# Folding a batch norm's scale into the product that turns a tile, with its biases added to x on GpSimd

## The chip, the cores and the metric

The kernel runs on one core of a Trainium2 chip. The metric is the device time of one execution in microseconds; the median of three runs is given. Names of the engines in the profile: PE is TensorE (PEld its weight loads), DVE is VectorE, ACT is ScalarE, POOL is GpSimd, SP is SyncE, which here only issues transfers.

## What is computed

A graph with 6250 nodes of 256 features and 100000 edges goes through an attention layer and then through three GIN layers. Cut to what matters around the change:

```python
h = relu(layernorm(x))
a = attention(h, edges)            # weights per edge, sums per node
h = batch_norm(h + a @ Wo + bo, bn1_g, bn1_b)
h2 = relu(h @ W1 + b1) @ W2 + b2
x = x + batch_norm(h + h2, bn2_g, bn2_b)      # bn2: this and the next line
h = relu(layernorm(x))                        # are the changed stage
for w, b in ((w1, b1), (w2, b2), (w3, b3)):   # GIN, relu after the first two
    h = ((1 + eps) * h + segment_sum(h[src], dst)) @ w + b
out = x + h
```

The batch norm takes its mean and variance over the nodes, one pair for each feature, and is then one multiplication and one addition: h * r2 + m2, with r2 and m2 a number for each feature.

## The kernel before

The program first sorts out the edges into 53 chunks and computes the first layer norm and the three projections (stage 0); then it runs the function `chunked`:

- attention, chunk by chunk, with rows gathered by indirect transfers that GpSimd issues (`gather`, L396). Its result is `h_t`, kept in SBUF with the features on the partitions: 128 partitions, two halves of the features (index f), 6250 nodes along the free dimension;
- the dense stage (L811 to L835), in 13 parts of up to 512 nodes, that rewrites `h_t` in place and collects the statistics of the second batch norm;
- `batchnorm("bn2", ...)` (L795 to L807), which leaves `r2` and `m2`, one column for each half of the features;
- the changed stage (L838 to L863), called s1c here;
- three passes over the 53 chunks, one for each GIN layer. In each, `neighbours` gathers 15 tiles of 128 rows for a chunk (L893, issued at L396) and sums them with a one-hot product on PE (L894). The first pass reads the table `g0_d` in DRAM, which s1c writes.

s1c works on ten blocks of 5 x 125 = 625 nodes. A block's x is loaded with one row of 256 features for each node (`xg`: 125 partitions, 5 rows each, 3 buffers). `h_t` has the features on the partitions, so each tile of 125 nodes has to be turned: for each half f, ACT computes hn = h_t * r2 + m2 (L847), PE transposes hn against the identity `ident` into the PSUM tile `tp` (L854, 4 buffers), and DVE adds `tp` to `xg` (L855). `layernorm` then takes bn_stats and bn_aggr for each of the five rows on DVE (L150, L151), a square root on ACT and a reciprocal on DVE (L141, L142) and one scalar_tensor_tensor on DVE (L154). ACT writes relu(x * r + m) to `g0` (L860, five times). `xg` goes to `x1_d` and `g0` to `g0_d`.

Every load and store of a block is issued by `halves` (L129 to L132) in two parts, 112 and 13 partitions (SPLIT = 112), 560 and 65 KB. Loads of x and stores of x1 are issued by SP, stores of g0 by ACT. A scheduler sets the order in which each engine gets its instructions; within one engine they run in that order. For SP in s1c it is: loads of blocks 0 and 1; store 0; the large part of load 2; store 1; the small part of load 2; load 3; load 4; stores 2 and so on, with a load waiting until its buffer, used three blocks before, has been stored and read.

Of the kernel before, what the change touches and what calls it, by code (L numbers as in the profile page):

```python
# [27 lines left out]
FT = mybir.dt.float32  # L28
BF = mybir.dt.bfloat16
I32 = mybir.dt.int32  # L30
AF = mybir.ActivationFunctionType
OP = mybir.AluOpType
# [5 lines left out]
P = 128  # L38
NN = 6250
NE = 100000  # L40
D = 256
# [4 lines left out]
FB = 125  # L46
# [41 lines left out]
def gnn_kernel(ctx: ExitStack, tc: tile.TileContext, a: dict, out: bass.AP):  # L88
# [266 lines left out]
    with branch.Else():  # L355
        chunked(tc, a, out, t)
# [3 lines left out]
def chunked(ctx, tc, a, out, t):  # L360

    nc = tc.nc
    iota, iota_p, ident = t.iota, t.iota_p, t.ident
# [431 lines left out]
    def batchnorm(name, stats):  # L795

        g = column(wp, name + "_g", a[f"L0_gnn_{name}_g"], 2)
        b = column(wp, name + "_b", a[f"L0_gnn_{name}_b"], 2)
        mv = wp.tile([P, 2, 2], FT, name=name + "_mv")
        for f in range(2):  # L800
            nc.vector.bn_aggr(mv[:, f, :], stats[:, f].rearrange("p c k -> p (c k)"))
        r = t.rsqrt(wp, name + "_r", mv[:, :, 1], 2)
        nc.vector.tensor_tensor(r, r, g, op=OP.mult)
        m = wp.tile([P, 2], FT, name=name + "_m")
        nc.vector.tensor_tensor(m, mv[:, :, 0], r, op=OP.mult)
        nc.vector.tensor_tensor(m, b, m, op=OP.subtract)
        return r, m  # L807

    r1, m1 = batchnorm("bn1", stats1)
    with tc.tile_pool(name="s1b", bufs=2) as sp, tc.tile_pool(name="s1b_ps", bufs=4, space=PSUM) as pp:  # L810
        for n, (c0, w) in enumerate(parts):  # L811
# [4 lines left out]
            for f in range(4):  # L816
                ps = pp.tile([P, 512], FT, name="ps")
                for k in range(2):
# [4 lines left out]
                        start=k == 0,  # L823
                        stop=k == 1,
                    )
                nc.scalar.activation(hid[:, f, :w], ps[:, :w], AF.Relu, bias=b_1[:, f : f + 1])
            for f in range(2):
# [6 lines left out]
                nc.vector.scalar_tensor_tensor(to, ps[:, :w], b_2[:, f : f + 1], to, op0=OP.add, op1=OP.add)  # L834
                nc.vector.bn_stats(stats2[:, f, n, :], to)  # L835

    r2, m2 = batchnorm("bn2", stats2)
    with tc.tile_pool(name="s1c", bufs=2) as sp, tc.tile_pool(name="s1c_ps", bufs=4, space=PSUM) as pp:  # L838
        for b0 in range(0, NFB, 5):
            xg = sp.tile([P, 5, D], FT, name="xg", bufs=3)  # L840
            halves(nc.sync, lambda s: xg[s], lambda s: rows_of(a["x"], b0, 5)[s])
            for k in range(5):
                b = b0 + k
                hn = sp.tile([P, 2, FB], FT, name="hn")
                tp = pp.tile([P, D], FT, name="tp")
                for f in range(2):
                    nc.scalar.activation(  # L847
                        hn[:, f, :],
                        h_t[:, f, b * FB : (b + 1) * FB],
                        AF.Identity,  # L850
                        bias=m2[:, f : f + 1],
                        scale=r2[:, f : f + 1],
                    )
                    nc.tensor.transpose(tp[:FB, f * P : (f + 1) * P], hn[:, f, :], ident)  # L854
                nc.vector.tensor_tensor(xg[:FB, k, :], xg[:FB, k, :], tp[:FB, :], op=OP.add)  # L855
            r, m = t.layernorm(sp, [xg[:FB, k, :] for k in range(5)], 5)
            halves(nc.sync, lambda s: rows_of(x1_d, b0, 5)[s], lambda s: xg[s])
            g0 = sp.tile([P, 5, D], FT, name="g0")
            for k in range(5):
                nc.scalar.activation(  # L860
                    g0[:FB, k, :], xg[:FB, k, :], AF.Relu, bias=m[:FB, k : k + 1], scale=r[:FB, k : k + 1]
                )
            halves(nc.scalar, lambda s: rows_of(g0_d, b0, 5)[s], lambda s: g0[s])  # L863
# [926 lines left out]
```

## Time and profile before

| what | us |
|---|---|
| median of three runs | 5583.78 |
| their lowest and highest | 5550.34, 5595.96 |
| the profiled execution, device time | 4526.41 |
| its span, first to last instruction | 4524.6 |
| mean granted TensorE clock in it | 0.803 |
| dense stage, 1217 to 1395 | 178 |
| s1c, 1395 to 1478 | 83 |
| the three passes, 1478 to 4524 | 3046 |

The profiled execution is shorter than the timed runs by 1057 us. A profile shows one execution, and all durations below come from it. PEclk is the clock that TensorE was granted, as a share of the full one; a row such as "x100 | 42.6, 571 | 34.0" gives the number of instructions, their busy time in us, the mean of one in ns, and the idle time of the engine just ahead of them with what ended it. Buffer numbers are left out of names, and where a helper issues a transfer, its line is the helper's (L132 for all of `halves`).

### The profile page before, as it was taken

What the parts mean: (1) busy time and instruction counts of PE and PEld (TensorE: products, weight loads), DVE (VectorE), ACT (ScalarE), POOL (GpSimd) and SP (SyncE); (2) the same over time, 40 slices, a digit from 0 to 9 for tenths busy, and PEclk for the clock granted to TensorE, in tenths of its full rate; (3) what the DMA queues carried; (4) which work ended last, traced back from release to release, by engine and by line L of the source; (5) the groups of instructions that cost most, each with busy time, mean ns of one, the idle gap of its engine ahead of it and who ended that gap; (6) DMA issues with size and microseconds to landing.
All of it is one profiled execution on the core that took longest, in us unless ns stands there. A gap on an engine that the chain in (4) does not pass through costs nothing. (4 is left out here: it accounts for less than half of the span.)

```text
span 4524.6 us, 36719 instructions
## 1 busy us (share of the span) xinstructions
PE 3645.1 (81%) x11051; PEld 1912.4 (42%) x11051; DVE 1486.8 (33%) x3034; ACT 746.2 (16%) x1610; POOL 3020.7 (67%) x3186
## 2 busy tenths in 40 slices
PE   7666666666696678877887899999999888888888
PEld 4344444444444334433333344444444333333333
DVE  6577777777724111111111121212121111111110
ACT  2244444444326000000000001010101000000000
POOL 0277777777300777777776777777776677777776
PEclk9888888888896787788777999999999666555555
DMA  4555555555205444444443777777776333333333
GB/s 126 145 150 152 152 152 153 152 152 152 68 1 159 148 126 125 126 126 126 126 126 114 224 243 232 242 231 243 231 243 202 100 112 112 112 112 112 112 112 104
DMA packets 315949, 671.18 MB, mean 148 GB/s; under 512 B 79412, under 2 KB 166734, under 8 KB 315743
## 3 DMA queue, kind: packets, MB, share of 16 engines
q0 software_dynamic: 178080, 524.47, 39.6%
q1 hardware_dynamic: 114005, 126.08, 9.2%
q10 hardware_dynamic: 23658, 18.21, 1.4%
q8 instruction: 89, 1.46, 0.1%
q14 instruction: 117, 0.96, 0.1%
HBM read 614.38 MB, written 54.13 MB: 148 GB/s over the span
## 5 line engine op out<-in xcount | busy, mean ns | idle before, releaser
L894 PE MATMUL sum<-g,hot 128*128 128x256 f32 (+1 forms) x4770 | 2282.1, 598 | 385.0 <-DMA g<-g_d,src_t 236.1
L396 POOL DMA_INDIRECT g<-g_d,src_t x1590 | 1510.5, 950 | 788.0 <-issue 491.9
L894 PEld LDWEIGHTS sum<-g,hot 128*128 128x128 f32 x4770 | 983.2, 240 | 1593.3 <-DMA g<-g_d,src_t 576.2
L396 POOL DMA_INDIRECT g<-vs_d,src_t x795 | 755.9, 951 | 431.7 <-issue 221.0
L396 POOL DMA_INDIRECT g<-y_d,src_t x795 | 753.8, 948 | 274.0 <-issue 233.5
L696 PE MATMUL acc<-g,hot 128*128 128x264 f32 x1590 | 509.5, 466 | 62.7 <-DVE g L686 61.5
L696 PEld LDWEIGHTS acc<-g,hot 128*128 128x128 f32 x1590 | 343.1, 232 | 127.2 <-DVE g L686 74.3
L413 DVE TENSOR_TENSOR hot<-ruler,loc_t 128x1920 f32<-128x1920 f32 x159 | 341.6, 2150 | 11.9 <-DMA g_d<-g 10.0
L1012 DVE TENSOR_TENSOR o<-sum,base 128x256 f32<-128x256 f32 (+1 forms) x53 | 22.5, 425 | 868.3 <-PE sum L894 868.3
L525 PE MATMUL flip<-ident,s_e 128*120 128x128 f32 x53 | 24.7, 465 | 343.3 <-ACT s_e L520 343.3
L686 DVE TENSOR_TENSOR g<-g,at_ps 128x1024 f32<-128x1024 f32 x212 | 239.5, 1151 | 14.9 <-ACT at_ps L677 8.5
L936 DVE SCALAR_TENSOR_TENSOR own<-own,eps,sum 128x256 f32<-128x256 f32 (+1 forms) x53 | 25.5, 480 | 525.6 <-PE sum L894 525.6
L966 PE MATMUL h_ps<-tt,g_w 128*128 128x512 f32 (+1 forms) x448 | 190.8, 570 | 0.6 <-ACT tt L954 0.6
L525 PEld LDWEIGHTS flip<-ident,s_e 128*120 128x120 f32 x53 | 9.2, 174 | 353.7 <-ACT s_e L520 353.7
L1000 DVE SCALAR_TENSOR_TENSOR own<-own,eps,sum 128x512 f32<-128x512 f32 (+1 forms) x53 | 39.5, 746 | 347.4 <-PE sum L894 347.4
L918 ACT COPY tt<-tp 128x256 f32<-128x256 f32 (+1 forms) x53 | 19.7, 372 | 736.5 <-PE tp L917 736.5
L925 DVE TENSOR_TENSOR g<-h_ps,g_b 128x512 f32<-128x512 f32 (+1 forms) x53 | 36.7, 692 | 304.1 <-issue 273.1
L954 ACT COPY tt<-tp 128x512 f32<-128x512 f32 (+1 forms) x53 | 31.0, 585 | 611.3 <-PE tp L953 581.0
L985 DVE SCALAR_TENSOR_TENSOR base<-y,eps,x 128x256 f32<-128x256 f32 (+1 forms) x53 | 25.5, 486 | 315.0 <-ACT y L980 313.7
L966 PEld LDWEIGHTS h_ps<-tt,g_w 128*128 128x128 f32 x448 | 82.7, 190 | 100.3 <-issue 99.5
L492 DVE TENSOR_TENSOR hot<-ruler,loc_t 128x1024 f32<-128x1024 f32 x106 | 117.3, 1148 | 5.8 <-ACT ruler L407 5.8
L506 ACT ACTIVATE hot_t<-loc_r,minus_p 128x896 bf16<-128x896 bf16 x106 | 115.6, 1090 | 8.9 <-DMA loc_r<-loc_d 8.9
(161 smaller groups left out, 2718.5 us busy)
## 6 DMA issues: line engine op xcount, KB each, us to landing
loc_r<-loc_d SPq DMA_DIRECT2D x53, 480.0 KB
g<-g_d,src_t POOLq DMA_INDIRECT x1590
g_d<-g SPq DMA_DIRECT2D x52, 256.0 KB
own<-g_d SPq DMA_DIRECT2D x52, 256.0 KB
g<-vs_d,src_t POOLq DMA_INDIRECT x795
g<-y_d,src_t POOLq DMA_INDIRECT x795
xg<-in_x_dram SPq DMA_DIRECT2D x20, 560.0 KB
own<-vs_d SPq DMA_DIRECT2D x52, 132.0 KB
```

The lines of the kernel that those rows point to most:

```text
L396: nc.gpsimd.indirect_dma_start(out=to, out_offset=None, in_=table, in_offset=bass.IndirectOffsetOnAxis(ap=src_c[:, c, j : j + 1], axis=0),)
L413: nc.vector.tensor_tensor(hot, rule[:, None, :P].to_broadcast([P, CK, P]), loc_c[:, c, :][:, :, None].to_broadcast([P, CK, P]), op=OP.is_e ...
L492: nc.vector.tensor_tensor(s.hot[:, js, :], rule[:, None, :P].to_broadcast([P, n, P]), loc_c[:, s.c, js][:, :, None].to_broadcast([P, n, P] ...
L506: nc.scalar.activation(s.hot_t[:, edges_of(q)], s.loc_r[:, edges_of(q)], AF.Square, bias=minus_p)
L525: nc.tensor.transpose(s.flip[: CK * H, :P], s.s_e.rearrange("p j h -> p (j h)"), ident)
L686: nc.vector.tensor_tensor(rows, rows, s.w_e[:, j0 // 8, j0 % 8 : j0 % 8 + n, :, None].to_broadcast([P, n, H, C]), op=OP.mult,)
L696: nc.tensor.matmul(s.acc, s.hot[:, j, :], s.g[:, j, :], start=j == 0, stop=j == CK - 1)
L894: nc.tensor.matmul(ps, hot[:, j, :], g, start=j == 0, stop=j == CK - 1)
L925: nc.vector.tensor_tensor(g1[R], h_ps[R], g_b1[R], op=OP.add)
L954: nc.scalar.copy(tt[:, :, q, R], tp[:, :, R])
L966: nc.tensor.matmul(h_ps[:, :n], g_w2[:, k, f * P : (f + 1) * P], tt_f[:, k, :n], start=k == 0, stop=k == 3)
L1000: nc.vector.scalar_tensor_tensor(own[R], own[R], eps1[R, 1:2], ps[R], op0=OP.mult, op1=OP.add)
```

## The change

The scale leaves ACT: a 128 x 128 diagonal matrix for each half, `scales` (the identity times r2), becomes the moving operand of the product that turns the tile, and `h_t` itself its stationary one, so that the product is h_t transposed and scaled. It is a product of f32 numbers now, no longer a transpose. The addition of m2 leaves ACT too: a product of a matrix of ones with a second diagonal matrix, `biases`, gives a tile that holds m2 as a row on every partition; ACT copies it to SBUF once (`bias`), and GpSimd adds it to each block of x, all five rows in one instruction of 125 x 1280, ahead of DVE's addition. `hn` is gone, `xg` has four buffers in place of three. All other lines of the stage stay as they were.

```diff
     r2, m2 = batchnorm("bn2", stats2)
     with tc.tile_pool(name="s1c", bufs=2) as sp, tc.tile_pool(name="s1c_ps", bufs=4, space=PSUM) as pp:
+        scales = sp.tile([P, 2, P], FT, name="scales", bufs=1)
+        biases = sp.tile([P, 2, P], FT, name="biases", bufs=1)
+        for f in range(2):
+            nc.vector.tensor_scalar(biases[:, f, :], ident, m2[:, f : f + 1], None, op0=OP.mult)
+            nc.vector.tensor_scalar(scales[:, f, :], ident, r2[:, f : f + 1], None, op0=OP.mult)
+        bias_ps = pp.tile([P, D], FT, name="bias_ps", bufs=1)
+        nc.tensor.matmul(bias_ps, t.ones, biases.rearrange("p f n -> p (f n)"), start=True, stop=True)
+        bias = sp.tile([P, D], FT, name="bias", bufs=1)
+        nc.scalar.copy(bias, bias_ps)
         for b0 in range(0, NFB, 5):
-            xg = sp.tile([P, 5, D], FT, name="xg", bufs=3)
+            xg = sp.tile([P, 5, D], FT, name="xg", bufs=4)
             halves(nc.sync, lambda s: xg[s], lambda s: rows_of(a["x"], b0, 5)[s])
+            nc.gpsimd.tensor_tensor(xg[:FB], xg[:FB], bias[:FB, None, :].to_broadcast([FB, 5, D]), op=OP.add)
             for k in range(5):
                 b = b0 + k
-                hn = sp.tile([P, 2, FB], FT, name="hn")
                 tp = pp.tile([P, D], FT, name="tp")
                 for f in range(2):
-                    nc.scalar.activation(
-                        hn[:, f, :],
+                    nc.tensor.matmul(
+                        tp[:FB, f * P : (f + 1) * P],
                         h_t[:, f, b * FB : (b + 1) * FB],
-                        AF.Identity,
-                        bias=m2[:, f : f + 1],
-                        scale=r2[:, f : f + 1],
+                        scales[:, f, :],
+                        start=True,
+                        stop=True,
                     )
-                    nc.tensor.transpose(tp[:FB, f * P : (f + 1) * P], hn[:, f, :], ident)
                 nc.vector.tensor_tensor(xg[:FB, k, :], xg[:FB, k, :], tp[:FB, :], op=OP.add)
```

In the order of SP's queue after the change, the large part of load 2 comes ahead of store 0; its small part stays behind store 1, and the pattern is then: stores of blocks 2k and 2k+1, the small part of load 2k+2, load 2k+3, the large part of load 2k+4. PE builds the tiles of a block in the order of the blocks as before, with the bias product in between those of the first tiles. On POOL the ten adds stand behind the last gather of attention and ahead of the first of the GIN passes.

## The prediction

> **What bounds the kernel now.** I began with the page. Its chain that ended last is of no use here (every share in it is 0%), so I went by stage: the busy time of each engine in five stretches, cut where the timeline shows one stage end and the next begin.
>
> ```profile
> 1217.00:1395.00 178.00, 170.31 (x417) 77.03 (x416) 52.51 (x96) 36.66 (x56) 0.00 (x0) 0.98 0.01 2
> 1395.00:1478.00 83.00, 42.62 (x100) 28.21 (x100) 44.70 (x171) 66.82 (x162) 0.00 (x0) 0.51 0.79 229
> 1478.00:2480.00 1002.00, 777.57 (x1905) 384.55 (x1906) 171.30 (x159) 52.44 (x105) 754.00 (x795) 0.78 0.43 127
> ```
>
> The columns are the stretch, its length, the busy time of PE, PEld, DVE, ACT and POOL, the granted clock, the DMA share and GB/s. The changed stage is the second row: 83 of 4524.6 us, 1.8% of the span. No engine is full in it; ACT (66.8) is nearest, DMA is at 0.79, POOL does nothing. What follows waits for all of it: the first gather of the next pass reads rows that any block may have written.
>
> ```profile
> 1478.95 0.95 POOL L396 DMA_INDIRECT g<-g_d,src_t  x1 [290.19 <-issue]
> ```
>
> POOL had idled 290 us when the last row landed, so a microsecond saved in this stage moves the three passes behind it forward one for one. Inside the stage, the groups:
>
> ```profile
> L854 PE MATMUL tp<-ident,hn 128*125 128x128 f32 x100 | 42.6, 571 | 34.0 <-ACT hn L847 33.8
> L847 ACT ACTIVATE hn<-h_t,bn_m,bn_r 128x125 f32<-128x125 f32 x100 | 40.6, 479 | 3.9 <-ACT hn L847 3.0 <-DVE bn_m L806 0.9
> L860 ACT ACTIVATE g<-xg,ln_m,ln_r 125x256 f32<-125x256 f32 x50 | 25.5, 585 | 1.6 <-DMA g_d<-g 1.1 <-DVE ln_m L154 0.5
> L855 DVE TENSOR_TENSOR xg<-xg,tp 125x256 f32<-125x256 f32 x50 | 20.3, 412 | 28.0 <-PE tp L854 24.4 <-DMA g_d<-g 2.0 <-DMA xg<-in_x_dram 1.3
> ```
>
> PE waits 33.8 us for ACT's hn, and DVE waits 24.4 us for PE: ACT is the head of the chain. Its queue, one period of it:
>
> ```profile
> 1434.50 5.11 ACT L847 ACTIVATE hn<-h_t,bn_m,bn_r 128x125 f32<-128x125 f32 x13 [0.69 <-ACT hn L847]
> ...
> 1440.91 2.55 ACT L860 ACTIVATE g<-xg,ln_m,ln_r 125x256 f32<-125x256 f32 x5
> 1443.37 0.48 ACT L847 ACTIVATE hn<-h_t,bn_m,bn_r 128x125 f32<-128x125 f32 x1
> 1443.49 0.86 ACTq L132 DMA_DIRECT2D g_d<-g  x2
> 1445.65 0.30 ACT L141 ACTIVATE ln_r<-ln_mv,eps 125x5 f32<-125x5 f32 x1 [1.80 <-DVE ln_mv L151]
> ...
> 1450.16 5.11 ACT L847 ACTIVATE hn<-h_t,bn_m,bn_r 128x125 f32<-128x125 f32 x13 [0.61 <-ACT hn L847]
> ```
>
> The pattern repeats every two blocks, 1450.16 - 1434.50 = 15.66 us: 20 hn at 0.39 (5.11 / 13) = 7.9, ten L860 = 5.1, and the rest square roots, the issue of stores, and 1.8 of waiting. SP's own queue gives the same period from the stores of x1:
>
> ```profile
> 1404.89 0.84 SPq L132 DMA_DIRECT2D x_d<-xg  x2
> 1405.77 8.75 SPq L132 DMA_DIRECT2D xg<-in_x_dram  x5
> ...
> 1422.95 0.98 SPq L132 DMA_DIRECT2D x_d<-xg  x2
> ```
>
> Block 1's store starts at 1404.89, block 3's at 1422.95, block 9's at 1469.67: four pairs in 64.8 us, 16.2 each (the first is 18.1).
>
> **The change part by part.**
> Removed: 100 ACT instructions L847, 40.6 us. ACT keeps 67 - 41 = 26 us and stops being the head.
>
> Moved to PE: 100 transposes become 100 f32 products of a 128x125 stationary tile with a 128x128 moving one. An f32 product is two records, as in
>
> ```profile
> 1202.90 1.05 PE L751 MATMUL dense<-att_t,w_o 128*128 128x128 f32 x8
> ```
>
> that is 0.26 us a product at the clock of 0.83 to 1 there, 0.52 for a node tile of two; the two transposes that it replaces take 0.38 in the same stretch (L740). What the clock will be is the open question. In the trace it falls from 0.98 in the dense stage to 0.50 in this one, although PE was busy 6.98 of 8 us in one stretch. [...] Against it stands the last pass: true f32 products, PE busy 858.0 us in the 984 from 3540 to 4524, clock 0.57. I take that row: 0.52 / 0.57 = 0.92 us a tile; the ends are 0.52 and 1.05 (clock 0.50).
>
> Added once: four DVE builds of 128x128 (L100, the same shape: 0.27 each), of which about 0.8 lie ahead of the bias, a 128x256 product (0.5 to 1), a PSUM copy on ACT (0.37, L918). bn_m is ready at 1395.1 in the trace, so the bias is there at about 1397.3.
>
> Added on POOL: ten adds of 125x1280. No row shows a POOL add. Below, the nearest row is DVE's 128x1920 add at 2.15 us (L413), so 1.43. [...] I take 2.8, with 1.4 and, were it twice as slow, 5.6 as ends. All ten are 28 us on an empty engine, but each stands between a load and DVE's add.
>
> Does the add block DVE? [...] by the order on the queues, close to none: L154 of an even block runs among the adds of the odd one, whose POOL add is done, and L154 of an odd block about 2.5 us after the last add, when the next load is still under way. I take 0, with 5 us as the upper end. The trace has no POOL compute here to show it.
>
> Queues. SP's order is kept in kind: store of 2k-1 (two issues), the 13-row part of load 2k, load 2k+1. The fourth xg buffer lets the big part of load 2 go at once and loads wait for an older block's ACT; but the small part of load 2k stays behind the store of block 2k-1, so POOL's add of 2k waits for it. That is the new chain, per pair:
> - store issue 0.86 (row above), then 3.7 from the load's issue at 1405.77 to the DVE add that it let start, at 1409.45;
> - POOL add 2.8, hand-over 0.1;
> - DVE's ten adds of the pair. Four tiles lie ready in PSUM; the other six come at PE's pace: 0.4 + 6 x 0.92 + 0.4 = 6.3. At full clock DVE itself binds: 5.6 (the pitch inside its bursts: adds 10 x 0.35, bn_stats 5 x 0.33, bn_aggr 5 x 0.1).
>
> Together 13.8 us, against 16.2. At clock 0.50 14.6; at full clock 13.1. DMA sets a floor: 3.84 MB a pair, and the stretch 1411 to 1419 moved 304 GB/s at a share of 1.01, so 12.6. Behind the store, block 2k-1's bn_stats, bn_aggr, L154 and L860 run under the 7.5 us of load and POOL add; without that cover they would add about 2.5.
>
> The start gets later: the first add waits for bias and POOL, 1397.3 + 0.1 + 2.8 = 1400.2 where it was 1397.93; the store of block 1 comes at about 1407.1 instead of 1404.89, +2.2. The tail behind the last store (1469.67 to 1478) has no L847 in it: unchanged. After the stage POOL is free, so its gathers are not held.
>
> Sum: 4 x (16.2 - 13.8) = 9.6 saved, 2.2 lost: -7 us. The profiled execution, 4526.4 us with 1.8 outside its span, becomes 4519. The timed runs' median, 5583.8, is 1057 us above it, and no trace of a timed run is shown. A lower clock would fit; this stage already ran at 0.51 and is held by ACT, POOL and DMA, so I carry -7 over: 5577.
>
> **The rivals.**
> 1. No gain: POOL's add and the load's latency take what ACT gave back (period 15.5 to 16.5). For it: DMA at 0.79 on average, loads behind 560 KB stores on the same queue. Against it: DVE's 24.4 us of waiting for PE. 5584.
> 2. Slower: the POOL add in the load chain. The period is 11.0 plus the add, so it passes 16.2 at 5.2 us an add, 1.9 times my value. At 8 us an add the period is 19: 4 x 2.8 + 2.2 + 5.2 at the start = +19, 5603. Against it: [...] and DVE's own row at 1.43.
> 3. Full gain: clock back to 1, DVE the limit at 13.1 with DMA close under it: 4 x 3.1 - 2 = -10, down to -12 at DMA's 12.6; 5573. [...] against it the last pass's clock.
>
> That the change does not shorten ACT at all is excluded: L847 is gone.
>
> **How the numbers follow.** Forecast (-2 to -9) 0.55, rival 3 0.15, rival 1 0.2, rival 2 0.1. All four lie within 1% (56 us), about the least that a measurement of this kernel can tell from no change: the three runs alone spread over 46 us. To leave that band on the fast side the stage would have to shrink from 83 to 27 us, while its 19.2 MB need 63 at 304 GB/s. So only a shift of the granted clock between runs can do it: faster 0.07, same 0.89, slower 0.04. The mechanisms span 5571 to 5603; the median of new runs scatters by some 20 us besides: 5545 to 5603.
>
> **What would show it.** Right: the stage from bn_m to the first gather at about 76 us; ACT about 26 us busy; DVE waiting for POOL or for a load once per pair rather than for PE; POOL adds near 2.8 us; x1 stores of odd blocks some 13.8 us apart. Wrong: POOL adds above 5 us; L154 stretched to microseconds; a granted clock near 1 (then rival 3); or x1 stores still 16 us apart.

## The result, and the profile after

| | median us | lowest to highest | runs |
|---|---|---|---|
| before | 5581.61 | 5549.89 to 5595.96 | 14 |
| after | 5579.74 | 5551.36 to 5596.67 | 14 |

The ratio of the two times is 1.0001, with a 95% interval of 0.9984 to 1.0017: no difference that the whole time can show. The stage itself does show one, and it is not the forecast one. I measure the stage from the start of the instruction that completes m2 (L806) to the first gather behind it (L396). Before, that is 1394.9 to 1478.9, 84.0 us. After, it is 1841.1 to 1927.5, 86.4 us, where about 76 were forecast.

The profiled execution of after has a span of 5576.1 us and everything ahead of the stage is later in it than in the one of before, so only distances within the stage can be compared. These are its busy times by stretch (columns as in the prediction: stretch, length, PE, PEld, DVE, ACT, POOL, granted clock, DMA share, GB/s):

```profile
1841.00:1927.00 86.00, 35.70 (x202) 33.57 (x202) 43.46 (x176) 29.25 (x63) 28.78 (x10) 0.71 0.78 222
```

ACT fell from 66.8 to 29.3 us, as the diff says, and the granted clock rose from 0.51 to 0.71. No engine is full; the DMA share is what it was (0.78), because the same bytes go through in nearly the same time. The end of the stage, on GpSimd's queue:

```profile
1927.54 0.96 POOL L396 DMA_INDIRECT g<-g_d,src_t  x1 [14.02 <-DMA g_d<-g]
```

The first gather still waits for the last row of `g0` to land. The groups of the stage say who waits now:

```profile
L858 PE MATMUL tp<-scales,h_t 128*125 128x128 f32 x200 | 35.2, 351 | 41.4 <-DVE xg L865 38.8 <-DVE bn_m L806 2.6
...
L853 POOL TENSOR_TENSOR xg<-xg,bias 125x1280 f32<-125x1280 f32 x10 | 28.8, 2886 | 271.1 <-DMA xg<-in_x_dram 267.1 <-DVE ln_st L150 3.5 <-DMA g_d<-g 0.5
L870 ACT ACTIVATE g<-xg,ln_m,ln_r 125x256 f32<-125x256 f32 x50 | 25.7, 588 | 8.2 <-DVE ln_m L154 5.8 <-DMA x_d<-xg 1.5 <-DMA xg<-in_x_dram 0.5
...
L865 DVE TENSOR_TENSOR xg<-xg,tp 125x256 f32<-125x256 f32 x50 | 18.7, 413 | 30.8 <-POOL xg L853 30.3 <-PE tp L858 0.3
...
L141 ACT ACTIVATE ln_r<-ln_mv,eps 125x5 f32<-125x5 f32 x10 | 3.0, 300 | 42.1 <-DVE ln_mv L151 42.1
```

The chain has been turned round. DVE, which waited 24.4 us for PE, waits 0.3 us for PE and 30.3 us for GpSimd's bias add; ACT, which had been the head, waits 42.1 us for DVE; PE waits 38.8 us for DVE to free `tp`. GpSimd in turn waits for loads of x (most of the 267.1 us is the idle time ahead of the stage). So DVE traded 24 us of waiting for ACT and PE against 30 us of waiting for a load and the add behind it.

### The profile page after: what moved, and what is told of

Its sections match the earlier page's. It is cut to its first block, busy times and chain, and to the rows that moved or that the text cites. A ratio compares the mean times of both kernels' runs of the same rounds, so it can differ in the third digit from the quotient of the medians.

```text
span 5576.1 us, 36825 instructions
## 1 busy us (share of the span) xinstructions
PE 3347.2 (60%) x11153; PEld 2033.7 (36%) x11153; DVE 1479.7 (27%) x3038; ACT 711.7 (13%) x1511; POOL 3046.8 (55%) x3196
## 4 chain that ended last, share of the span: by engine, by line
PE 40%; another core or an unknown queue 28%; issue 17%; DVE 9%; ACT 3%; DMA 2%; POOL 1%; SPq 0%; DVEq 0%; ACTq 0%; POOLq 0%
PE sum L904 23%; PE h_ps L976 3%; PE acc L696 3%; PE qk_ps L330 2%; PE h_ps L933 2%; PE y_ps L986 2%; PE ps L819 2%; PE ps L830 2%; DVE g L686 1%; DVE hot L492 1%; DVE ruler L650 1%; PE v_ps L332 1%; ACT hot_b L500 1%; DVE hot L413 1%
## 5 line engine op out<-in xcount | busy, mean ns | idle before, releaser
L904 PE MATMUL sum<-g,hot 128*128 128x256 f32 (+1 forms) x4770 | 1821.7, 525 | 512.6 <-issue 453.6
L396 POOL DMA_INDIRECT g<-g_d,src_t x1590 | 1503.6, 946 | 971.1 <-PE sum L904 370.5
L904 PEld LDWEIGHTS sum<-g,hot 128*128 128x128 f32 x4770 | 1044.8, 226 | 1217.2 <-issue 1054.6
L396 POOL DMA_INDIRECT g<-vs_d,src_t x795 | 762.8, 960 | 849.6 <-issue 229.3
L396 POOL DMA_INDIRECT g<-y_d,src_t x795 | 751.1, 945 | 422.4 <-issue 210.5
L696 PE MATMUL acc<-g,hot 128*128 128x264 f32 x1590 | 567.0, 503 | 537.9 <-DVE g L686 304.4
L696 PEld LDWEIGHTS acc<-g,hot 128*128 128x128 f32 x1590 | 374.9, 253 | 617.3 <-DVE g L686 311.0
L927 PE MATMUL tp<-ident,own 128*128 128x128 f32 (+1 forms) x106 | 29.0, 366 | 438.8 <-DVE own L946 325.1
L976 PE MATMUL h_ps<-tt,g_w 128*128 128x512 f32 (+1 forms) x448 | 213.3, 624 | 101.7 <-issue 68.8
L933 PE MATMUL h_ps<-g_w,tt 128*128 128x512 f32 (+1 forms) x212 | 151.2, 852 | 151.9 <-issue 82.8
L927 PEld LDWEIGHTS tp<-ident,own 128*128 128x128 f32 (+1 forms) x106 | 15.0, 175 | 453.7 <-DVE own L946 334.4
L853 POOL TENSOR_TENSOR xg<-xg,bias 125x1280 f32<-125x1280 f32 x10 | 28.8, 2886 | 271.1 <-DMA xg<-in_x_dram 267.1
```

The source lines that it names most:

```text
L396: nc.gpsimd.indirect_dma_start(out=to, out_offset=None, in_=table, in_offset=bass.IndirectOffsetOnAxis(ap=src_c[:, c, j : j + 1], axis=0),)
L696: nc.tensor.matmul(s.acc, s.hot[:, j, :], s.g[:, j, :], start=j == 0, stop=j == CK - 1)
L904: nc.tensor.matmul(ps, hot[:, j, :], g, start=j == 0, stop=j == CK - 1)
L933: nc.tensor.matmul(h_ps[R], tt[:, f, R], g_w1[:, f, :], start=f == 0, stop=f == 1)
L976: nc.tensor.matmul(h_ps[:, :n], g_w2[:, k, f * P : (f + 1) * P], tt_f[:, k, :n], start=k == 0, stop=k == 3)
```

## The experiments

Theory A: the chain store, load, bias add, DVE, next store holds the stage, and the load in it takes longer than the 3.7 us that I gave it, because it is issued behind stores. Theory B: something else takes the gain (too few buffers, the tiles' pace on PE, or that the order alone, not the change, is what matters). The table gives the stage of each run, and the whole time beside the median of before in the same job (before and the other kernels of a job run on the same chip). The stage is read from one trace for each run; the whole time is a median of 22 executions in e4 and of 13 in e5 and e8, and one execution in the others.

| run | L806 to first gather | stage us | whole us | before us |
|---|---|---|---|---|
| e1_before_again | 1837.3 to 1921.3 | 84.0 | 5570.40 | 5572.82 |
| e2_bufs6 | 1822.5 to 1909.7 | 87.2 | 5551.63 | 5572.82 |
| e3_no_add | 1837.9 to 1911.4 | 73.5 | 5572.77 | 5572.82 |
| e4_x1_act | 1841.9 to 1929.0 | 87.1 | 5577.12 | 5572.82 |
| e5_ahead | 1394.2 to 1466.5 | 72.3 | 4505.52 | 4516.09 |
| e6_before_ahead | 1392.1 to 1475.0 | 82.9 | 4513.25 | 4516.09 |
| e7_twice_add | 1393.5 to 1499.1 | 105.6 | 4537.23 | 4516.09 |
| e8_after_again | 1392.5 to 1479.0 | 86.5 | 4523.69 | 4520.63 |
| e9_ahead_no_add | 1395.2 to 1465.5 | 70.3 | 4505.16 | 4520.63 |

**e1_before_again**: before, unchanged.

> The kernel before once more, for a trace of its stage beside those of the variants. The stage (bn_m to the first gather of the first GIN pass) is held by ACT and DMA, not by what makes whole executions 4526 or 5580 us long: 83 us as in the first trace (82 to 85). If instead the first trace caught the stage in a favourable moment, it is 88 us or more here, and the changed kernel's 86 us would be a gain hidden by the comparison of two different executions.

Its stage took 84.0 us, the same as in the first profile, in an execution of 5570.4 us. The program of before thus takes 4516 to 4521 us in some jobs and about 5570 in others; here the extra 1044 us lie ahead of the stage (it begins 442 us later) and behind it (602 us), none in it. So the stage can be compared across jobs, and whole times only within one.

**e8_after_again**: after, unchanged, in a job in which before takes 4520.6 us. It gives the trace of after that stands nearest to the first one of before, so I read the mechanism there.

> The changed kernel once more, unaltered, timed beside the one before. Theory (what ACT gave up comes back as POOL's add, and the start gets 2 us later): the stage is 86 us as in its first trace, against 84, so the whole is 1 to 4 us longer, ratio 1.0003 to 1.0009. Rival (the first trace was unlucky and the change does save what the sum said): stage 75 to 78 us, ratio 0.998.

The stage was 86.5 us again, the ratio 1.0007 (0.9998 to 1.0015). SP's queue in it (start, length, line, output and input, number of issues):

```profile
1401.03 4.91 SPq L132 DMA_DIRECT2D x_d<-xg  x4
1405.98 4.34 SPq L132 DMA_DIRECT2D xg<-in_x_dram  x4
1414.78 6.84 SPq L132 DMA_DIRECT2D x_d<-xg  x4
1421.68 6.20 SPq L132 DMA_DIRECT2D xg<-in_x_dram  x4
1432.49 4.58 SPq L132 DMA_DIRECT2D x_d<-xg  x4
1437.12 6.17 SPq L132 DMA_DIRECT2D xg<-in_x_dram  x4
1448.17 5.11 SPq L132 DMA_DIRECT2D x_d<-xg  x4
1453.33 4.05 SPq L132 DMA_DIRECT2D xg<-in_x_dram  x3
```

The stores of two blocks, then loads, in turn; each group of loads starts as the one of stores ends. GpSimd's adds in the same trace, with the wait ahead of them in brackets:

```profile
1409.65 2.88 POOL L853 TENSOR_TENSOR xg<-xg,bias 125x1280 f32<-125x1280 f32 x1 [8.03 <-DMA xg<-in_x_dram]
1415.92 2.88 POOL L853 TENSOR_TENSOR xg<-xg,bias 125x1280 f32<-125x1280 f32 x1 [3.38 <-DMA xg<-in_x_dram]
1427.36 5.87 POOL L853 TENSOR_TENSOR xg<-xg,bias 125x1280 f32<-125x1280 f32 x2 [8.56 <-DMA xg<-in_x_dram]
1443.04 5.84 POOL L853 TENSOR_TENSOR xg<-xg,bias 125x1280 f32<-125x1280 f32 x2 [9.81 <-DMA xg<-in_x_dram]
1459.21 5.73 POOL L853 TENSOR_TENSOR xg<-xg,bias 125x1280 f32<-125x1280 f32 x2 [10.32 <-DMA xg<-in_x_dram]
```

The first load of a pair takes from its issue to the add that it lets start 1409.65 - 1405.98 = 3.67 us in the first pair, as I had taken it, and then 1427.36 - 1421.68 = 5.68, 1443.04 - 1437.12 = 5.92, 1459.21 - 1453.33 = 5.88. In the first pair it is the second load that is late: its add starts 6.3 us behind the first one, at 1415.92. Busy times in the stretches between these marks, two of waiting for a load and two of computing:

```profile
1421.70:1427.40 5.70, 0.06 (x1) 0.00 (x0) 1.64 (x8) 3.54 (x8) 0.04 (x1) 0.77 0.99 283
1427.40:1437.10 9.70, 6.35 (x39) 6.36 (x40) 6.80 (x27) 2.15 (x5) 5.74 (x2) 0.61 0.76 230
1437.10:1443.00 5.90, 0.32 (x3) 0.13 (x2) 1.67 (x8) 3.58 (x8) 0.00 (x0) 0.90 0.97 277
1443.00:1453.30 10.30, 6.87 (x38) 6.87 (x39) 6.89 (x27) 2.67 (x6) 5.78 (x2) 0.56 0.73 216
```

While the load is waited for, the DMA engines are full (0.97 to 0.99, 277 to 283 GB/s) and PE, GpSimd and most of DVE stand still; while they compute, the transfers fall to 216 to 230 GB/s. The load that starts a pair is only the 13-row part of its block, 65 KB; the other 560 KB were issued one group earlier. On SP's queue it stands right behind the x1 store of the odd block, and 0.2 to 0.7 us after it ACT issues the store of the even block's `g0`. In the second pair, from 1424.0 to 1426.5, the two queues moved (packets, MB, share of the engines; q10 is ACT's queue and q1 is SP's):

```profile
q10 hardware_dynamic: 583, 0.58, 78.9%
q1 hardware_dynamic: 139, 0.12, 19.8%
```

From 1421.7 to 1423.5, just before, it was q1 alone, 0.50 MB. So the small load waits for one block's x1 store and then for most of a `g0` store that was issued after it. From its issue until it has landed, at 1427.20, the engines move 1.55 MB in all, 0.64 of them `g0`; in the first pair it is 0.96 MB, 0.26 of them `g0`. The 3.7 us of the prediction had been read in before, where the store of `g0` had not set in: 0.01 MB on q10 from 1405.77 to 1409.45. This sharing is read from the traces; no run takes the stores of `g0` away.

**e2_bufs6**: more buffers for x, to see whether loads wait for them.

```diff
-            xg = sp.tile([P, 5, D], FT, name="xg", bufs=4)
+            xg = sp.tile([P, 5, D], FT, name="xg", bufs=6)
```

> The changed kernel with six xg buffers in place of four. Theory (order): the small part of load 2k stands behind the store of block 2k-1 on SP's queue, whatever the buffers; stage 86 us, loads still 15 to 17 us apart. Rival (buffers): loads wait for a buffer to come free; with two more, the stage falls by 5 us or more.

87.2 us, as the theory of the order had it, and the order of SP's queue was the one of after: the small part of load 2k still stood behind the store of block 2k-1. In that order the load stands behind the store, whatever buffer is free. Buffers alone are not the cause.

**e3_no_add**: the ten bias adds are left out, and with them m2 from the result.

```diff
-            nc.gpsimd.tensor_tensor(xg[:FB], xg[:FB], bias[:FB, None, :].to_broadcast([FB, 5, D]), op=OP.add)
```

> The changed kernel without the ten adds of the bias on POOL: this leaves the batch norm's bias m2 out of the result. Theory (the add is in series with load and DVE): each pair gets shorter by one add, 15.9 - 2.9 = 13.0 us, the stage by 2.9 for each of five pairs and the start, about 14 to 17 us, to 70 to 72. Rival (transfers bind, the add is hidden under them): 83 to 86 us.

The stage fell to 73.5 us, 12.9 less than in after and a little above the 70 to 72 expected. Its SP queue:

```profile
1861.21 4.26 SPq L132 DMA_DIRECT2D xg<-in_x_dram  x4
1869.11 5.11 SPq L132 DMA_DIRECT2D x_d<-xg  x4
1874.27 4.43 SPq L132 DMA_DIRECT2D xg<-in_x_dram  x4
1882.31 5.11 SPq L132 DMA_DIRECT2D x_d<-xg  x4
1887.47 4.04 SPq L132 DMA_DIRECT2D xg<-in_x_dram  x3
```

The period is 13.1 us (1861.21 to 1887.47 is two), against 15.8 in e8 (1421.68 to 1453.33 is two), so nearly all of one add of 2.9 us per pair stands in the chain. The load's term is still there: from its issue to DVE's first add it took 5.7, 5.9 and 6.3 us in the last three pairs. From the first odd store to the last it is 53.0 us here and 63.0 in e8, and the first one comes 9.3 us behind L806 here and 12.6 in e8. That start is not the add alone, since the order of the first transfers changed too (here store 0 goes ahead of the large part of load 2). Without the add the scale in the product alone would have given the stage 10.5 us.

**e4_x1_act**: the stores of x1 leave SP's queue, so that loads no longer stand behind them.

```diff
-            halves(nc.sync, lambda s: rows_of(x1_d, b0, 5)[s], lambda s: xg[s])
+            halves(nc.scalar, lambda s: rows_of(x1_d, b0, 5)[s], lambda s: xg[s])
```

> The changed kernel with the stores of x1 issued by ACT in place of SP, so that no load stands behind a store. Theory (order): loads run ahead by four buffers, POOL's add is done before DVE wants the block, and the period falls to the DMA floor of about 12.6 us a pair (DVE needs about 9): stage 70 to 74 us, 12 to 16 us saved, ratio about 0.9975. Rival (DMA rate binds already, 3.84 MB a pair at the measured mean of 222 GB/s): stage 83 to 87 us, ratio 1.000.

A miss: 87.1 us, ratio 1.0011 (0.9995 to 1.0026). Loads did come free: DVE's wait for the adds fell to 17.4 us. But all stores now shared the queue of ACT, and two other waits grew (engine, what it waits for, us in total, times, longest):

```profile
ACT g L870 <- DVE ln_m L154: 37.4, 8, 7.2
...
POOL g L396 <- DMA g_d<-g: 21.7, 1, 21.7
DVE xg L865 <- POOL xg L853: 17.4, 5, 5.7
```

Two stretches behind DVE's last add, and an issue of ACT:

```profile
1911.00:1913.50 2.50, 0.00 (x0) 0.00 (x0) 1.09 (x7) 1.79 (x5) 0.00 (x0) 0.50 0.00 1
1913.50:1917.70 4.20, 0.00 (x0) 0.00 (x0) 0.00 (x0) 1.80 (x4) 0.00 (x0) 0.50 1.00 295
...
1919.44 1.93 ACTq L132 DMA_DIRECT2D x_d<-xg  x2
```

Nothing is left to multiply. The stores move at 295 GB/s while there are any, and in between nothing is under way. The last line is the x1 store of the last block: DVE's last add ended at 1909.37, but ACT issued the store ten us later, behind the L870 and the stores of the block before it on its own queue. So the time that the loads gained went into ACT's queue, and not into slower stores.

**e5_ahead**: after, with the loads issued three blocks ahead and the adds two, so that neither stands behind a store that is still to come.

```diff
-        for b0 in range(0, NFB, 5):
-            xg = sp.tile([P, 5, D], FT, name="xg", bufs=4)
+        xs = []
+        def load(b0):
+            xg = sp.tile([P, 5, D], FT, name="xg", bufs=5)
             halves(nc.sync, lambda s: xg[s], lambda s: rows_of(a["x"], b0, 5)[s])
+            xs.append(xg)
+        def add_bias(xg):
             nc.gpsimd.tensor_tensor(xg[:FB], xg[:FB], bias[:FB, None, :].to_broadcast([FB, 5, D]), op=OP.add)
+        for b0 in range(0, 5 * 3, 5):
+            load(b0)
+        for n in range(2):
+            add_bias(xs[n])
+        for b0 in range(0, NFB, 5):
+            if b0 + 5 * 3 < NFB:
+                load(b0 + 5 * 3)
+            if b0 + 5 * 2 < NFB:
+                add_bias(xs[b0 // 5 + 2])
+            xg = xs[b0 // 5]
```

> The changed kernel with the loads of x written three blocks ahead and POOL's adds two blocks ahead of their use, and five xg buffers: on SP's queue each load now stands before the store of the block three earlier, and both parts of it together. Theory (the add costs time only because the load that feeds it stands behind a store): POOL's adds are done early, DVE no longer waits for POOL, the period falls to the transfers' 12.6 to 13.2 us a pair, the stage to 68 to 74 us from 86, and some 10 to 16 us come off the whole, ratio 0.997 to 0.998. Rival (any POOL add delays DVE, or the transfers are just as slow in another order): stage 82 us or more, ratio 1.000.

The stage took 72.3 us, and the whole 4505.52 against 4516.09, ratio 0.9978 (0.9970 to 0.9986): 10.6 us, the only one of the timed kernels whose interval excludes 1. The stage's row:

```profile
1394.20:1466.50 72.30, 36.47 (x202) 34.05 (x202) 47.90 (x176) 28.82 (x63) 28.75 (x10) 0.69 0.92 263
```

The adds cost GpSimd the same 28.75 us as before and the products PE the same 36; only their order against the transfers is new, and one buffer more (with six buffers and the old order, e2 gained nothing). DVE waits 12.9 us for GpSimd in place of 30, and the DMA share went from 0.78 to 0.92.

**e6_before_ahead**: the same lines for the loads in before (no adds, `hn` still on ACT), to see whether the order alone brings this.

> The kernel before with the same loads three blocks ahead and five buffers, L847 on ACT as before. Theory (ACT is the head of that kernel's chain): ACT's 67 us busy plus ten times 0.86 of issuing leave a floor of 75, with start and tail 78 to 82 us against 84. Rival (there too the order of the loads binds, and ACT's work fits beside it): 74 us or less, and then the change itself is worth nothing even in the mended order.

82.9 us, 1.1 less than before and just above the 78 to 82 expected. With ACT as the head the order of loads has nothing to give; the waits say so:

```profile
PE tp L864 <- ACT hn L857: 29.6, 17, 2.8
...
DVE xg L865 <- PE tp L864: 27.2, 19, 3.3
```

So neither part alone does it: the change is worth 82.9 - 72.3 = 10.6 us with the loads ahead and -2.5 us with the order that it came in.

**e7_twice_add**: the bias is halved and added twice, to double what GpSimd does.

```diff
-        nc.scalar.copy(bias, bias_ps)
+        nc.scalar.mul(bias, bias_ps, 0.5)
...
             nc.gpsimd.tensor_tensor(xg[:FB], xg[:FB], bias[:FB, None, :].to_broadcast([FB, 5, D]), op=OP.add)
+            nc.gpsimd.tensor_tensor(xg[:FB], xg[:FB], bias[:FB, None, :].to_broadcast([FB, 5, D]), op=OP.add)
```

> The changed kernel with POOL's add done twice for each block, half of the bias each time. Theory (in series): 2.9 us more for the first add of each of five pairs, the second one's partly beside DVE: period 15.9 + 2.9 = 18.8, stage 86 + 14 to 17 = 100 to 103 us. Rival (beside the transfers): 86 to 90 us.

105.6 us. The direction is that of an add in series, the size is not a clean reading: the scheduler grouped three blocks where after has two,

```profile
1404.95 12.48 SPq L132 DMA_DIRECT2D x_d<-xg  x6
1417.48 11.85 SPq L132 DMA_DIRECT2D xg<-in_x_dram  x6
```

so more than the add changed in it (three of its ten L154 also lasted 2.1 us, each until the add beside it had ended, as the next section shows for e5). The place of the add is settled by e3 and e9, not by this run.

**e9_ahead_no_add**: e5_ahead without the bias adds.

> The kernel with loads three blocks ahead, without POOL's adds: the bias m2 is left out of the result. Theory (in the mended order the add stands beside the transfers): at most 3 us less than with the adds, stage 69 to 72 us against 72.3, most of it the first add at the start. Rival (each pair still pays for an add): about 60 us.

```profile
1395.20:1465.50 70.30, 34.33 (x202) 31.83 (x202) 43.45 (x176) 28.81 (x63) 0.02 (x1) 0.72 0.95 271
```

2.0 us less than with them, where the same adds cost 12.9 us in the order of after. Ten adds of 2.88 us are all but hidden once they run ahead, and the transfers, at a share of 0.95, are nearly full.

## Why the prediction came out as it did

The whole time fell where the forecast put it, but that was no test and in part luck: a stage of 84 us in 5580 can't move it by 1%, and the rivals' values lay in the same range. The stage is the test, and there the forecast's sum was -7 and the measured one +2.5. Rival 1 (no gain, period 15.5 to 16.5, GpSimd's add and the load taking what ACT gave) is what happened, with a period of 15.7. Step by step, from e8 against the first trace of before:

| step | forecast us | measured us |
|---|---|---|
| ACT's work gone | 67 to 26 | 66.8 to 29.2 |
| GpSimd add, each | 2.8 | 2.88 |
| start, L806 to store of block 1 | +2.2 | 10.0 to 12.6: +2.6 |
| load in the chain | 3.7 | 3.7 once, then 5.7 to 5.9 |
| from DVE's start to the next load's issue | 7.2 | 9.1, 6.9 and 7.4 in the first three pairs |
| four pairs | -9.6 | 64.8 to 63.0: -1.8 |
| tail, store of block 9 to first gather | 0 | 9.2 to 10.9: +1.7 |
| sum | -7 | +2.5 |

The step that failed is the term "then 3.7 from the load's issue at 1405.77 to the DVE add that it let start". It was one reading at the start of the stage, with the store of `g0` not yet under way, carried to all four pairs; in the three later ones the load waits for one block's x1 store and shares the DMA engines with another's `g0`, and takes 5.7 to 5.9. The three exceed the term by 6.4 us in all, of the 7.8 us by which the pairs missed; the first pair missed by 1.9 through its late second load, and the other terms give 0.5 back. I had checked the DMA floor (12.6 us a pair) as an average, and e5 and e9 come near it (shares of 0.92 and 0.95). What it hides is that in this order the transfers and the computing take turns: full for 6 us, three quarters full for 10. The chain's shape, who waits for whom, was right, and e3 shows that it is a chain: taking the add out of it gives the add back.

One term came out right by luck. The sum had 6.3 us for DVE's ten adds, six of them at PE's pace of 0.92 us a tile. In e8 they take 6.4 us in the third pair (1445.95 to 1452.37), but DVE waits only 0.43 us of that for PE; the rest is its own work, the even block's bn_stats and bn_aggr in between.

The tail was forecast as unchanged because no L847 lies in it; it grew by 1.7 us. The growth lies ahead of the last store of `g0`, which ACT issues 4.2 us behind the x1 store of block 9 in before (1473.91 - 1469.67) and 6.1 us behind it in e8 (1474.15 - 1468.08). From there to the first gather it is 5.0 and 4.9 us. In before, DVE waits for PE between the last block's adds and has only two bn_stats left behind the last add; in e8 all five are left.

Right were the terms for the engines. PE does not bind: DVE waited under 1 us for `tp`. The clock of 0.57 that I had taken from the last pass was right for the stretches in which the products run (0.56 and 0.61 above), but a product took 351 ns, 0.70 us a tile in place of 0.92. The clock of 1 in rival 3 was my assumption for this stage; in e8 it came only late in a burst (0.50 at first, 0.99 from about 1452, last section), for a mean of 0.69 over the stage in e8 and 0.71 in after, against 0.51 before. None of this matters when PE waits for DVE (38.3 us in e8). The add's price of 2.8 had no row of before to show it; 2.88 was measured, twice the 1.43 worked out from DVE's row.

That L154 would not be held by GpSimd's adds (0 taken, 5 as the end) was right for this order: the ten took 0.16 us each in after, and none of them started while an add ran. That an add could hold L154 at all was not shown by the trace of before, which has no add on GpSimd. In e5, where adds run ahead and so beside the layer norm, four of the ten started beside an add (they took 0.29, 2.32, 2.28 and 0.49 us), and each lasted until that add ended. The two longest, first on GpSimd's queue, then on DVE's:

```profile
1419.46 2.88 POOL L858 TENSOR_TENSOR xg<-xg,bias 125x1280 f32<-125x1280 f32 x1 [6.24 <-ACT g L886]
...
1437.46 2.88 POOL L858 TENSOR_TENSOR xg<-xg,bias 125x1280 f32<-125x1280 f32 x1 [5.52 <-DMA xg<-in_x_dram]
```

```profile
1420.04 2.32 DVE L154 SCALAR_TENSOR_TENSOR ln_m<-ln_mv,ln_r 125x5 f32<-125x5 f32 x1
...
1438.07 2.28 DVE L154 SCALAR_TENSOR_TENSOR ln_m<-ln_mv,ln_r 125x5 f32<-125x5 f32 x1
```

L154 lasts until the add ends, to 0.02 us: 1420.04 + 2.32 = 1422.36 and 1419.46 + 2.88 = 1422.34. L881 and L150 also ran beside adds (four L881 from 1400.60 in 1.41 us, among the adds from 1397.69 to 1409.14), and take 410 and 411 ns on average, as in e8 (412 and 410): they were not held. Why L154 is held and these are not, no run separates. In e5 the ten L154 take 6.3 us in place of 1.6.

The remark that a lower clock would explain the 1057 us between the profiled execution and the timed runs is not borne out. The granted clock is 0.756 to 0.766 in the long executions and 0.786 to 0.821 in the short ones, 5 to 7% apart in the means, and the times differ by 23%. What makes the rest stays open (each of the three jobs of the experiments ran on another chip, so that chip and job can't be told apart); both kernels show it.

## What to carry to other kernels

Taking work from the busiest engine gave nothing here (84.0 us before, 86.4 and 86.5 after), because the piece that replaced it stood in series behind a load, and the load behind a store on the same queue; look at what is issued ahead of the load that starts the chain, and issue loads a few blocks ahead before moving work (72.3 us in e5). Take a load's latency from a place where as much else is in flight as there will be (3.67 us in the first pair of e8, 5.7 to 5.9 in the later ones), and look at the DMA share in the waiting and in the computing part of a period apart, since an average of 0.78 was 0.97 to 0.99 and 0.73 to 0.76 in turn. The move of work lost 2.5 us alone and the change of order gained 1.1 alone, and together they took 11.7 us off the stage (84.0 to 72.3), so try the second before giving up the first.

## What was unexpected of the hardware

- The granted clock changed later than the products did. In e8, a burst of them runs from 1446.43 to 1453.8; the clock is 0.50 in it until about 1452, then 0.99, and it is 1.00 from 1456.5 to 1458, where no product runs:

```profile
1450.50:1452.00 1.50, 1.50 (x9) 1.50 (x9) 1.07 (x5) 1.07 (x3) 0.00 (x0) 0.50 0.51 163
1452.00:1453.50 1.50, 1.50 (x15) 1.50 (x15) 1.50 (x7) 1.50 (x4) 0.00 (x0) 0.99 0.12 38
1456.50:1458.00 1.50, 0.00 (x0) 0.00 (x0) 0.00 (x0) 1.50 (x5) 0.00 (x0) 1.00 1.03 276
```

  In after it is the same in the burst from 1878.65 to 1885.5: 0.50 until 1883, 0.93 and then 1.00 in it, and 1.00 from 1887 to 1889, where no product runs. So of the four stretches above the two with the products have the lower means (0.61 and 0.56, against 0.77 and 0.90). With transposes, before, the mean over the stage was 0.51.
- A load of 65 KB took 5.7 to 5.9 us from its issue to the add that waited for it (e8), while a store of 0.64 MB ahead of it on its queue and one that another queue had got later went through.
